# When blocks are closed, when an image's first keys are fetched, and where the routing's chain stands: three edits of order in a fused convolution, state-space, attention and expert kernel

## The chip, the cores and the metric

The kernel runs on one core of one Trainium2 chip. The metric is the device time of one execution in microseconds (us). Matrix products run on TensorE (PE), elementwise work and scans on VectorE (DVE), activations on ScalarE (ACT), a few powers and fills on GpSimd (POOL); SyncE (SP) issues the DMAs of the main loop.

## The reference, cut to what matters

Two layers over `x` of shape (4, 128, 64, 64): four images of 4,096 tokens with 128 channels, all in float32.

```python
# layer 0: group norm, depthwise 3x3 convolution, a Mamba scan over the tokens (4 chunks of channels)
x = x + conv_block(gn(x))
...
def step(h, inp):                       # for each of 4096 tokens
    dA_t, dBu_t, C_t = inp
    h = dA_t * h + dBu_t                # di = 64, N = 16
    y = jnp.einsum('bdn,bn->bd', h, C_t)
    return (h, y)
...
# layer 1: attention with 4 heads of 32, then 8 experts of which 2 are taken
t = to_tokens(x)
t = t + attention(ln(t))                # softmax(q k^T / sqrt(128)) v, then W_proj
n = ln(t)
p = softmax(n @ router_w + router_b)
top_p, top_i = top_k(p, 2);  top_p = top_p / sum(top_p)
t = t + sum_k top_p[k] * (n @ expert_w[top_i[k]] + expert_b[top_i[k]])
```

## The kernel before, in words

All of it is one loop (L1362) whose order is written out by hand. The program is built by Python generators; each engine's instructions are chained in the order in which they are recorded (`queued`, L389), so the order is fixed when the program is built and does not depend on time.

An image's tokens are cut into 8 blocks of 512 (`BLK`), so there are 32 blocks, (image b, block i). The scan of a block takes 2 halves of the channels (p) times 8 pairs of states; each such unit takes two turns of the loop, called steps here (`slot`). A block of the scan is thus 32 steps, and the scan ends after step 1,023. Block number k begins at step 32k. A step issues the fetch of the scan's rows from DRAM, one `da` activation for a later unit, in an even step the product `h` and the scan, in an odd step the product `hc`, and the transposes `y` of an earlier one.

Beside the scan, each step takes one attention group if there is one (L1383): two tiles of 128 keys against 1,024 queries of one head, 4 matmuls into `sc`, two exponentials into `pT`, and, in the next step, the matmuls into `av`. The groups of an image come from `attention(b)` (L912): the runs in `RUNS` (L903) name a pair of query blocks and a range of key blocks, each run goes over the four heads, and is cut into parts of one or two key blocks. A part is loaded (`qs`, `ks`, `v`, from DRAM) during the last three groups of the part ahead of it (L954) if all blocks that it needs are closed (`ready`, L908); if that was not so, the generator gives None, a step without a group, until they are, then loads, and gives None twice more (L940 to L945). There is one generator for each image, and they run one after the other (L1333): the first part of an image always takes the second way. An image has 256 groups.

Everything else runs in two lanes, X and Y, each with a queue of tasks; a task is a generator whose pieces are recorded at two places of a step. The Y lane gives its pieces in the middle of a step (L1393, L1406), the X lane one at the end of a step (L1412) and one early in the next (L1382), ahead of the attention group and of the scan or `hc`. An X task begins at the end of a step. Y has the group norm, the first norm (`gn`, `y0`), the convolution (`xn`, on VectorE as nine taps for images 1 to 3) and the scan's inputs (`in`, which also use the X lane's PSUM bank for two products). X has two kinds of task:
- `closed(b, i)` (L793): after the scan of a block it makes the layer's output, normalises it, and writes keys, queries and values to DRAM. It takes 18 pieces, and is put at the head of X when the second half of the block has been summed up (`summed_up`, L778). That is early in step 3 of the block that follows.
- `("out", b, i)` (`finished`, L1032): after all keys of a pair of query blocks, it loads the sums (`aT`), the inverse denominators (`inv`) and the tokens (`acc`), projects, normalises, routes, and adds the 8 experts' products, whose weights (shares) come back from DRAM. It takes 30 pieces; it is put at the tail of X by the third of the steps of `inverted`, 8 steps after the last group of the pair.

A task, once begun, keeps its lane to its end. As long as the scan runs, an output may begin only in steps 2 to 17 of a block (L1268). Before the change the outputs of a steady block begin in step 2, so the closed task that comes in step 3 waits for piece 30 and begins in step 17.

In `finished`, the router's exponential is piece 12, piece 13 is empty, the choice of the two experts (17 small instructions on VectorE, called the routing's chain) is piece 14, and the transposes of `both` on TensorE are piece 15. Odd pieces stand at the end of a step, even ones early in the next. Each lane has one PSUM bank (`ps_X`, `ps_Y`). After the scan, outputs may begin in any step and on both lanes.

Of the kernel before, what the change touches and what calls it, by code (L numbers as in the profile page):

```python
# [24 lines left out]
NST = 16  # L25
# [11 lines left out]
def conv_mamba_attn_moe_kernel(ctx: ExitStack, tc: tile.TileContext, t: dict):  # L37
    nc = tc.nc
    x, out = t["x"], t["out"]
    B, _, L = x.shape  # L40
    NB = L // BLK
# [11 lines left out]
    def load(name, shape=None, src=None, eng=nc.sync, pool=const):  # L53
        src = t[name] if src is None else src
        w = pool.tile(list(shape or src.shape), F32, name=f"w_{name}")
        eng.dma_start(out=w, in_=src)
        return w
# [354 lines left out]
    def mm(out, lhsT, rhs, start=True, stop=True):  # L412
        tensor.matmul(out, lhsT=lhsT, rhs=rhs, start=start, stop=stop)
# [460 lines left out]
    def queries(b, qp, h):  # L874

        qs = att.tile([P, 2 * BLK], F32R, name="qs", bufs=2)
        src = kqv[b][1][qp][DH * h : DH * h + DH].rearrange("d a r l -> (d a r) l")
        sync.dma_start(out=qs.bitcast(F32), in_=src)
        return qs

    def keys(b, h, k, u, n):

        ks = att.tile([P, 2 * BLK], F32R, name="ks", bufs=3)
        src = kqv[b][0][k][DH * h : DH * h + DH].rearrange("d a l -> (d a) l")
        src = src[:, u * BLK : (u + n) * BLK]
        sync.dma_start(
            out=ks[:, : n * BLK].bitcast(F32),
            in_=src[:, None, :].to_broadcast([2 * DH, 2, n * BLK]),
        )
        return ks  # L890

    def values(b, h, k, u, n):
        v = att.tile([P, 2, NT, 2 * DH], F32, name="v", bufs=3)
        sync.dma_start(
            out=v[:, :n].rearrange("p i j d -> p i (j d)"),
            in_=kqv[b][2][k][h, u : u + n].rearrange("i p q -> p i q"),
        )
        return v
# [9 lines left out]
    def ready(b, part):  # L908
        last = max(2 * part[0] + 1, 2 * part[2] + part[3] + part[4] - 1)
        return all(("closed", b, i) in done for i in range(last + 1))  # L910

    def attention(b):  # L912

        seen, parts = {}, []
        for q, lo, hi in RUNS:
            known = seen.get(q, 0)
            seen[q] = known + hi - lo  # L920
            cuts = [lo, *range(lo + 2 - lo % 2, hi, 2), hi]
            for h in range(NH):
                for k0, k1 in zip(cuts, cuts[1:]):
                    parts.append((
                        q, h, k0 // 2, k0 % 2, k1 - k0, k0 == lo, k1 == hi, known > 0,
                        seen[q] == NB,
                    ))
        assert all(n == NB for n in seen.values())

        def load(part, qs=None):  # L930
            q, h, k, u, n = part[:5]
            if qs is None:
                qs = queries(b, q, h)
            return qs, keys(b, h, k, u, n), values(b, h, k, u, n)

        prev = None
        ahead = None
        for at, part in enumerate(parts):
            q, h, k, _, n, first, last, more, final = part
            if ahead is None:  # L940
                while not ready(b, part):
                    yield None
                ahead = load(part)
                for _ in range(2):
                    yield None  # L945
            qs, ks, v = ahead
            ahead = None
            for g in range(0, NT * n, STEP):
                if g == 0 and last:
                    prev = None  # L950
                    if more:
                        prev = att.tile([P, BLK], F32, name="prev", bufs=2)
                        sync.dma_start(out=prev, in_=partial.pop((b, q, h)))
                if g >= NT * n - 3 * STEP and ahead is None and at + 1 < len(parts):  # L954
                    nxt = parts[at + 1]
                    if ready(b, nxt):
                        ahead = load(nxt, qs if nxt[:2] == (q, h) and not nxt[5] else None)
                scs = []
                for j in range(g, g + STEP):
                    sc = ps_sc.tile([P, 2, BLK], F32, name="sc")  # L960
                    for u in range(2):
                        mm(
                            sc[:, u, :], ks[:, j * P : (j + 1) * P],
                            qs[:, u * BLK : (u + 1) * BLK],
                        )
                    scs.append((v[:, j // NT, j % NT, :], sc))
                yield (
                    b, q, h, scs, first and g == 0, last and g + STEP == NT * n, prev, final,
                )
# [62 lines left out]
    def finished(b, qb, lane):  # L1032

        q, u = divmod(qb, 2)
# [44 lines left out]
        yield  # L1079
        scalar.activation(pr, pr, AF.Exp)  # L1080
        yield
        yield

        revb = rev[:, None, :].to_broadcast(wide)

# [16 lines left out]
        vector.reciprocal(top1, top1)  # L1102
        vector.tensor_mul(both[:, :, 0:NE], pr, top1.to_broadcast(wide))
        vector.tensor_mul(both[:, :, NE:], both[:, :, 0:NE], rs[:, :, None].to_broadcast(wide))
        yield

        ps = work(lane)
# [9 lines left out]
        def share(e):  # L1117

            if lane == "X":
                w = side.tile([P, 2, BLK], F32, name="share", bufs=3)  # L1120
            else:
                w = mix.tile([P, 2, BLK], F32, tag="rows", name="share", bufs=4)
            sync.dma_start(
                out=w.rearrange("p k q -> p (k q)"),
                in_=shares[e : e + 2].rearrange("e q -> (e q)")[None].to_broadcast([P, 2 * BLK]),
            )
            return w
# [8 lines left out]
        ahead = deque(share(e) for e in (0, 2))  # L1136
# [117 lines left out]
    def advance(lane, second):  # L1254

        if inside[lane] != second:
            return False
        while True:
            if lane not in running:

                tasks = lanes[lane] if lanes[lane] or slot < END else lanes["X"]
                if tasks and lane == "Y" and tasks[0][0][0] == "closed":
                    return False
                if not tasks or not all(k in done for k in tasks[0][2]):
                    return False

                if (
                    tasks[0][0][0] == "out" and slot < END + 4  # L1268
                    and not 2 <= slot % (2 * NST) < NST + 2
                ):  # L1270
                    return False
                key, stages, _ = tasks.popleft()
                running[lane] = key, stages(lane) if callable(stages) else stages
            key, stages = running[lane]
            try:
                next(stages)
                inside[lane] = not second
                return True
            except StopIteration:
                assert not second  # L1280
                done.add(key)
                del running[lane]

    def until(key):
        while key not in done:
            flush()
            count = len(done)
            moved = [
                advance(*half) for half in (("X", True), ("Y", False), ("Y", True), ("X", False))
            ]  # L1290
            assert any(moved) or len(done) > count, key
            if ("y0", *blocks[1]) in done:
                next(weights, None)
# [17 lines left out]
    for k in range(-2, len(blocks)):  # L1311
        if 0 <= k:
            b, i = blocks[k]
            Y.append((("in", b, i, 1), inputs(b, i, 1), [("scan", *blocks[k - 1], 1)] if k else []))
        if k + 2 < len(blocks):
            b, i = blocks[k + 2]
            if k + 2 == 0 or i > 0:
                upper(k + 2)
        if 0 <= k + 1 < len(blocks):
            b, i = blocks[k + 1]  # L1320
# [10 lines left out]
    left = [None]  # L1331

    def attention_groups():  # L1333
        for b in range(B):
            yield from attention(b)
        left.clear()

    groups = attention_groups()
    units = [(b, i, p, n) for b, i in blocks for p in range(2) for n in range(0, NST, 2)]
    END = 2 * len(units)  # L1340

    rows, due, closing, y_of = {}, deque(), deque(), {}
    h_of, slot = {}, 0
# [18 lines left out]
    while (  # L1362
        slot < END or due or closing or summing or waiting or left or later or lanes["X"] or running
    ):
        at, odd = divmod(slot, 2)
# [10 lines left out]
        if unit and not odd:  # L1376
            h = h_of.pop(at)
            driven(unit, h, rows.pop((at, 0)))
        if summing:
            summed_up(*summing)  # L1380
            summing = None
        advance("X", True)  # L1382
        group = next(groups, None)  # L1383
        if group:
# [3 lines left out]
        if unit and odd:  # L1388
            hc = read(h, rows.pop((at, 1)))
            late = 2 * (unit[3] == 0)  # L1390
            due.append((slot + 1 + late, unit, 0, hc[:, 0, :], False))
            due.append((slot + 2, unit, 1, hc[:, 1, :], ends(unit)))
        advance("Y", False)  # L1393
        while closing and closing[0][0] <= slot:
            summing = turned_back(*closing.popleft()[1:])
# [133 lines left out]
```

## Time and profile before

| | |
|---|---|
| three runs | 5178.62, 5182.59, 5191.08 us (median 5182.59) |
| the profiled execution | 5183.13 us, of which the span of the profile 5180.9 us |
| granted TensorE clock, mean | 0.957 |
| attention groups, `pT` exponentials | 1,024, 2,048 |
| `pT`, mean of one on ScalarE | 1022 ns |
| scan on VectorE, mean of one | 2353 ns |
| `h`, `hc` on VectorE, mean of one | 1218, 1220 ns |
| HBM read and written | 967.22 MB, 143.39 MB |

Times on the page are of one profiled execution. Instructions of the main loop all carry the line of the helper that records them (L406), so they are told apart by tile names: `sc` and `av` are attention, `h`, `hc`, `y`, `da` the scan, `both` the routing, `share` the experts' weights, `hi` and `lo` the keys and queries of a closed task, `gn`, `xt`, `cm` the norms and the convolution. A name with X or Y at its end belongs to a lane. The page gives each engine's busy time and 40 slices of the span:

```profile
PE   4567898999999998899999999999999999999997
DVE  6987767877778887878788887888788877751332
ACT  4556777787787787688888787788777787656543
PEclk7778999999999999899999999999999999999998
```

The first quarter is image 0, where attention starts late; the last four or five slices come after the scan has ended and hold attention and outputs alone.

### The profile page before, as it was taken

How to read it: one execution, taken by the hardware profiler on the slowest of the kernel's cores; microseconds unless marked ns; L12 is line 12 of the kernel's file. 1: busy time of each engine (PE TensorE's matmuls, PEld its weight loads, DVE VectorE, ACT ScalarE, POOL GpSimd, SP SyncE). 2: the span in 40 equal slices, each digit the busy share in tenths (PEclk: the TensorE clock that was granted, in tenths of full speed). 3: DMA queues.
4: the chain of work that ended last, by engine and by line, in shares of the span. 5: the costliest groups of instructions: out<-in, count | busy, mean ns of one | idle time of the engine just before them, and what ended most of it. 6: DMA issues, size and time to landing. Idle time of an engine off the chain costs nothing.

```text
span 5180.9 us, 62597 instructions
## 1 busy us (share of the span) xinstructions
PE 4710.1 (91%) x20684; PEld 2321.9 (45%) x20684; DVE 3835.8 (74%) x5780; ACT 3745.7 (72%) x5700; POOL 423.1 (8%) x483
## 2 busy tenths in 40 slices
PE   4567898999999998899999999999999999999997
PEld 2334444444444444444444444444444444443443
DVE  6987767877778887878788887888788877751332
ACT  4556777787787787688888787788777787656543
POOL 1111111100000000101000000000000001000000
PEclk7778999999999999899999999999999999999998
DMA  3556667677666766767766766777766666754542
GB/s 127 183 186 212 205 212 253 233 239 243 229 224 225 239 227 234 242 230 258 252 228 227 238 229 231 258 231 255 265 227 233 221 230 221 262 179 156 184 134 72
DMA packets 451693, 1131.70 MB, mean 218 GB/s; under 512 B 51858, under 2 KB 135331, under 8 KB 451363
## 3 DMA queue, kind: packets, MB, share of 16 engines
q1 hardware_dynamic: 447296, 1125.96, 64.3%
q8 instruction: 166, 2.72, 0.2%
q10 hardware_dynamic: 4066, 1.67, 0.1%
q14 instruction: 165, 1.34, 0.1%
HBM read 967.22 MB, written 143.39 MB: 214 GB/s over the span
## 4 chain that ended last, share of the span: by engine, by line
PE 59%; DVE 19%; ACT 10%; DMA 6%; issue 4%; POOL 2%; SPq 1%; DVEq 0%; ACTq 0%; POOLq 0%
PE av L406 25%; PE sc L406 14%; PE ps_X L406 9%; DVE h L406 6%; PE ps_Y L406 6%; PE y L406 5%; ACT pT L406 3%; ACT L406 2%; DVE hc L406 2%; DMA ks<-kd 2%; ACT xt L406 1%; DVE stX L406 1%; DVE du L406 1%; DMA rows<-bcd 1%; DVE cm L406 1%
## 5 line engine op out<-in xcount | busy, mean ns | idle before, releaser
L406 ACT ACTIVATE pT<-sc 128x1024 f32<-128x1024 f32 x2048 | 1984.3, 1022 | 934.3 <-PE sc L406 932.8
L406 PE MATMUL av<-pT,v 128*64 128x512 f32 x8192 | 2002.8, 610 | 10.8 <-DVE avs L406 10.8
L406 PE MATMUL sc<-qs,ks 128*128 128x512 f32 x4096 | 1302.7, 437 | 75.9 <-ACT pT L406 39.4
L406 DVE TENSOR_TENSOR_SCAN h<-da,state,h 128x1025 f32<-128x1025 f32 x512 | 1204.5, 2353 | 96.6 <-ACT h L406 62.8
L406 PEld LDWEIGHTS sc<-qs,ks 128*128 128x128 f32 x4096 | 703.1, 190 | 812.7 <-ACT pT L406 273.2
L406 PEld LDWEIGHTS av<-pT,v 128*64 128x64 f32 x8192 | 500.4, 137 | 845.7 <-issue 816.7
L406 ACT ACTIVATE da<-delta,amat 128x512 f32<-128x512 f32 x1024 | 742.9, 730 | 1.9
L406 PE MATMUL y<-ident,hc 128*128 128x128 f32 x4096 | 626.2, 284 | 64.6 <-DVE hc L406 64.6
L406 DVE TENSOR_TENSOR hc<-rows,h 128x1024 f32<-128x1024 f32 x512 | 624.6, 1220 | 15.3 <-PE y L406 5.4
L406 DVE TENSOR_TENSOR h<-rows,du 128x1024 f32<-128x1024 f32 x512 | 623.9, 1218 | 13.0 <-DMA rows<-bcd 8.5
L406 PEld LDWEIGHTS y<-ident,hc 128*128 128x128 f32 x4096 | 524.2, 147 | 229.0 <-issue 80.8
L406 ACT ACT_TABLE_LOAD x319 | 409.3, 1283 | 19.5 <-DVE zs L406 14.3
L406 POOL TENSOR_TENSOR rsX<-rsX,mhalf 128x4 f32<-128x4 f32 x92 | 203.7, 2214 | 2504.4 <-DVE rsX L406 2420.4
L406 POOL TENSOR_TENSOR rsY<-rsY,mhalf 128x4 f32<-128x4 f32 x100 | 130.7, 1307 | 2072.5 <-DVE shiftY L406 1561.5
L406 DVE TENSOR_TENSOR avs<-av,prev 128x512 f32<-128x512 f32 x96 | 66.2, 689 | 256.7 <-PE av L406 235.0
L406 PE MATMUL ps_X<-share,w_ew 128*128 128x512 f32 x432 | 213.9, 617 | 9.1 <-DVE share L406 8.8
L406 ACT ACTIVATE xt<-ps_Y,shiftY,rsY 128x128 f32<-128x128 f32 x380 | 143.6, 468 | 81.7 <-POOL shiftY L406 73.8
L406 DVE TENSOR_TENSOR share<-share,xf 128x1024 f32<-128x1024 f32 x128 | 156.0, 1219 | 16.5 <-DMA share<-sharesX 11.7
L406 ACT COPY state<-h 128x2 f32<-128x2 f32 x448 | 88.8, 198 | 92.0 <-DVE h L406 92.0
L406 DVE SCALAR_TENSOR_TENSOR cm<-y,w_fc1w,cm 128x512 f32<-128x512 f32 x195 | 145.1, 744 | 8.0 <-ACT y L406 4.5
L406 PE MATMUL ps_Y<-pairs,inxc 128*128 128x512 f32 x256 | 132.6, 643 | 15.5 <-DMA pairs<-xn 9.9
L406 PEld LDWEIGHTS ps_X<-share,w_ew 128*128 128x128 f32 x432 | 73.2, 189 | 147.0 <-issue 97.1
(248 smaller groups left out, 3437.2 us busy)
## 6 DMA issues: line engine op xcount, KB each, us to landing
rows<-bcd SPq DMA_DIRECT2D x1024, 512.0 KB
ks<-kd SPq DMA_DIRECT2D x192, 512.0 KB
qs<-qd SPq DMA_DIRECT2D x161, 512.0 KB
share<-sharesX SPq DMA_DIRECT2D x108, 512.0 KB
v<-vd SPq DMA_DIRECT2D x192, 256.0 KB
ks<-kd SPq DMA_DIRECT2D x128, 256.0 KB
avd<-avs SPq DMA_DIRECT2D x96, 256.0 KB
prev<-avd SPq DMA_DIRECT2D x96, 256.0 KB
```

Of the source, the lines that this page charges most:

```text
L406: return lambda *args, **kw: queued(op(*args, **kw))
```

## The change

Three edits. The generators of the images become one: `parts_of(b)` lists the parts of an image, `attention()` goes over the parts of all images, and each part carries its image, so the first part of an image can be loaded during the last groups of the image ahead of it by the same rule as any other. In the routing, the empty piece ahead of the chain is taken out and one is put behind it, so that the chain is piece 13 and the transposes stay piece 15. The steps in which an output may begin while the scan runs become 4 to 17.

```diff
-    def attention(b):
+    def parts_of(b):
...
                     parts.append((
-                        q, h, k0 // 2, k0 % 2, k1 - k0, k0 == lo, k1 == hi, known > 0,
-                        seen[q] == NB,
+                        b, (q, h, k0 // 2, k0 % 2, k1 - k0, k0 == lo, k1 == hi, known > 0,
+                            seen[q] == NB),
                     ))
         assert all(n == NB for n in seen.values())
+        return parts
+
+    def attention():
+
+        parts = [part for b in range(B) for part in parts_of(b)]
 
-        def load(part, qs=None):
+        def load(b, part, qs=None):
...
-        for at, part in enumerate(parts):
+        for at, (b, part) in enumerate(parts):
...
-                    nxt = parts[at + 1]
-                    if ready(b, nxt):
-                        ahead = load(nxt, qs if nxt[:2] == (q, h) and not nxt[5] else None)
+                    to, nxt = parts[at + 1]
+                    if ready(to, nxt):
+                        ahead = load(to, nxt, qs if nxt[:2] == (q, h) and not nxt[5] else None)
...
         scalar.activation(pr, pr, AF.Exp)
         yield
-        yield
 
         revb = rev[:, None, :].to_broadcast(wide)
...
         vector.tensor_mul(both[:, :, NE:], both[:, :, 0:NE], rs[:, :, None].to_broadcast(wide))
+        yield
         yield
...
                     tasks[0][0][0] == "out" and slot < END + 4
-                    and not 2 <= slot % (2 * NST) < NST + 2
+                    and not 4 <= slot % (2 * NST) < 18
...
     def attention_groups():
-        for b in range(B):
-            yield from attention(b)
+        yield from attention()
         left.clear()
```

More of the change, by code (lines that the diff above doesn't have):

```diff
@@ L942, in attention @@
                     yield None
-                ahead = load(part)
+                ahead = load(b, part)
                 for _ in range(2):
```

## The prediction

> **What bounds the kernel now.** I read the page first, then the busy time of TensorE in stretches of 32 steps, then TensorE's waits, then single places in the timeline. On the page TensorE is busy 91% of the span and leads the chain that ended last:
>
> ```profile
> PE 4710.1 (91%) x20684; PEld 2321.9 (45%) x20684; DVE 3835.8 (74%) x5780; ACT 3745.7 (72%) x5700; POOL 423.1 (8%) x483
> PE 59%; DVE 19%; ACT 10%; DMA 6%; issue 4%; POOL 2%; SPq 1%; DVEq 0%; ACTq 0%; POOLq 0%
> ```
>
> Each step issues one `da` activation (two more ahead of step 0), so the start of a 32-step block can be read off the timeline of `da`; counting the turns of the loop tells which steps have an attention group. Busy time in such stretches (us; TensorE busy; granted clock; DMA share; GB/s):
>
> ```profile
> 1219.70:1375.30 155.60, 143.91 (x642) 0.97 0.74 255
> 1664.40:1804.90 140.50, 126.03 (x567) 0.95 0.71 236
> 1804.90:1948.30 143.40, 140.00 (x642) 1.00 0.69 230
> 1948.30:2104.40 156.10, 129.79 (x544) 0.86 0.75 258
> 2249.70:2393.80 144.10, 140.47 (x642) 1.00 0.72 244
> 2393.80:2532.70 138.90, 131.44 (x600) 0.99 0.76 259
> 2825.40:2968.50 143.10, 134.55 (x618) 1.00 0.66 223
> 2968.50:3113.40 144.90, 141.45 (x647) 1.00 0.70 240
> 3113.40:3269.40 156.00, 143.50 (x630) 0.96 0.74 258
> 4001.80:4145.00 143.20, 135.30 (x613) 0.99 0.67 224
> 4145.00:4290.60 145.60, 140.89 (x642) 1.00 0.68 234
> 4690.00:4800.00 110.00, 110.00 (x443) 1.00 0.47 158
> ```
>
> An ordinary block (blocks 13, 16, 21, 29: 143.4, 144.1, 144.9, 145.6; mean 144.5) has 140 to 141 us of TensorE work and some 3.5 us in which it waits. So nothing is gained unless a wait of TensorE goes. The last row is a stretch after the scan has ended: attention alone, never idle; its groups follow each other every 2.99 us. The waits of TensorE from 1219.7 to 4559.3 us (total, times, longest) begin so:
>
> ```profile
> PE ps_X L406 <- DVE bothX L406: 40.0, 20, 4.1
> PE sc L406 <- ACT pT L406: 23.1, 87, 1.4
> PE sc L406 <- DMA ks<-kd: 21.1, 12, 4.7
> PE ps_X L406 <- DVE lo L406: 17.4, 20, 2.6
> ```
>
> **Part one: the groups that move (an image's first keys; closed tasks at step 3).** Counting the loop's turns in both programs: before, attention gives no group in steps 383-384, 409-412, 469-476, 653-654 and 911-912, 18 in all; two at each change of image (L944), the others because a block was not closed. After, there is none of these, since the closed task starts at step 3 of a block in place of 17. The last group falls in step 1150 in place of 1168; the loop has 1,176 turns for 1,194. Matmuls, exponentials and loads are the same in number.
> - Gained: 18 tail steps of 2.99 us = -53.8.
> - Paid: the same 18 groups inside the scan's steps. Block totals price them: block 12 (five bare steps, 384 and 409-412) took 140.5 against 144.5, so 4.0; block 11, with one, 142.5, so 2.0; blocks 20 and 28 143.1 and 143.2, so 1.4 and 1.3; block 14, with eight, took 156.1, and block 22, which has the same group norm and no bare step, 156.0: nothing. Together +8.7. The upper bound is from step to step: the 18 bare steps took 54.9 us (`da` to `da`), the same places of ordinary blocks some 83 by the means of 17 blocks: +28.
> - Sum -45.1, between -54 and -26. What goes is idle time in the bare steps, of which this wait (timeline) and this stretch at half clock (windows) are examples:
>
> ```profile
> 1793.21 1.11 PE L406 MATMUL y<-ident,hc 128*128 128x128 f32 x4 [6.67 <-DVE hc L406]
> 1666.40:1669.80 3.40, 3.13 (x10) 0.50 0.91 328
> ```
>
> **Part two: the routing's chain.** The chain (17 instructions on VectorE; in the timeline 1703.83 to 1707.37, 3.55 us) stood in step 9 after the VectorE work of step 8, and the transposes of `both` at the end of step 9 waited for it, 40.0 us in 20 blocks. Outputs now start at step 12 of the block, so the chain is queued at the end of step 18 and the transposes at the end of step 19. From the start of step 18 VectorE has `h` 1.22 + scan 2.35 + chain 3.55 = 7.1 us; TensorE has two steps of 3.42 (sc 1.2, y 0.6, av 1.94, overlapping) + `xt` 0.66 + `yT` 0.60 + fc2 1.2 = 9.3. The wait goes: -40.0, bounds -40 and 0. Without the moved yield `scanned` (0.73 + 0.69) would stand ahead: 8.5, still inside, so the half step alone is worth nothing here. On POOL the closed task's two powers move to steps 6 and 7 and the output's to 15; POOL is busy 8%, so only its latency counts, as in `xt` below. On SP's queue the output's share loads keep their distance to its own steps. Behind the chain on VectorE now stand `scanned` and `hc` of step 19 (done after 7.1 + 1.42 + 1.22 = 9.7); `hc` is read in step 20, after 9.3 + 0.65 + 1.2, and nobody waits.
>
> **Part three: what the closed task brings to steps 3 to 12.** Blocks 8, 9 and 17 have that order already. All three show the same stall in step 8:
>
> ```profile
> 2429.52 1.20 PE L406 MATMUL sc<-qs,ks 128*128 128x512 f32 x4
> 2432.81 0.66 PE L406 MATMUL ps_Y<-ident,gn 128*128 128x128 f32 x4 [2.09 <-DVE gn L406]
> ```
>
> In step 7 the closed task's `tt` and moments (2428.71 to 2431.08) and `hc` stand ahead of `gn`. There are 17 changed blocks with a `gn` there: 17 x 2.09 = +35.5 (0 if TensorE is later by then). The waits for `lo` (17.4), which come from closed tasks meeting `inputs` in steps 24 to 26, go, less 6.2 already counted in bare blocks: -11.2. In step 18 TensorE waits for `xt` 1.2 to 1.9 in the three blocks; the output's router matmuls (29.4 us / 27 = 1.09) now fill part of it: 0.5 x 20 = +10 (0 to 24). In blocks 14, 22, 30 VectorE has taps in steps 6 to 10; the 4.05 of `both` there is in the 40.0, and the closed task's 3.2 us of moments takes its place, up to 6 us: 3 x 3 = +9 (0 to 18).
>
> **Part four: just in time, and the clock.** The run that begins 80 groups into an image needs queries whose closed task ends in step 460, 716 or 972; they are asked for one step later and used in 463, 719, 975. Loads of `ks` took 7.05 and 8.15 us in the chain, after a write that must land first, against four steps of 3.4: +6, 0 to 15. As to the clock, each 3.4 us at half rate costs 1.7: `both` was followed by three such windows (4 in units of 3.4, -6.8), one stall for `gn` of three was (1260.2 to 1263.6, clock 0.50), so 17/3 x 1.7 = +9.6: +3 (0 to 20).
>
> [...]
>
> **Sum.** -45.1 - 40.0 + 35.5 - 11.2 + 10 + 9 + 6 + 3 = -32.8, on a profiled execution of 5183.1 (span 5180.9), which stands 0.5 above the median of the runs. Predicted: 5182.6 - 32.8 = 5149.8, taken as 5150. Likeliest case alone: 5122 to 5166. What a measurement of this kernel can tell from no change is about 0.3%, 15.5 us.
>
> **Rivals.**
> - *The exchange of order costs what the closed gaps give* (0.17). TensorE idles 8.4 and 7.5 us in blocks 8 and 17, which have the new order, against 3.5 in ordinary ones, without an output to carry. If the changed blocks idle 2 us more than before instead of my net 0.6 (12.3 / 22), 22 x 2 = 44 eats the 45: 5181.
> - *Slower: the output's first loads* (0.08). `aT`, `inv`, `acc` are issued after `hc` of step 11, and `aT x inv` waits for them on VectorE with the scan of step 14 behind it. Issue to product took 8.8 to 12.6 us; before, the steps 3 to 5 with `inputs` (5.3 us of TensorE) hid it, now steps 12 to 14 have three bare 3.42 = 10.3. At 4817.15 the same wait cost TensorE 4.09. It decides from landings of about 12 us on: 22 x 4.09 = 90, so 5182.6 - 33 + 90 = 5240. Against it: VectorE itself has two taps of 0.74 in step 11, then 1.2 + 0.7 + 2.35 + 1.5 in step 12, 1.2 + 1.5 in 13 and `h` 1.2 in 14, 11.1 us, before it gets there. On SP's queue the fetch of `rows` for step 13 stands behind these three loads, 0.5 us each to issue.
> - *More gain* (0.10, faster too): `gn` hidden and bare groups free, -54 - 40 - 11 = -105 at the most; half of the difference to mine gives 5114.
> - *The chain still waits* (0.05, within 0.3%): +40 on mine, 5190; the half step then did not do what it says. Against it stands the margin of 2.2 us above.
> - The forecast: 0.60. Faster than 5167: 0.60 + 0.10 + a part of the first rival (0.04) = 0.74; within 5167 and 5198: 0.13 + 0.05 = 0.18; slower: 0.08. The range for 8 in 10: 5116 (between more gain and mine) to 5181.
>
> **What would show it.** No step without a group after step 206: `pT` to the end of the scan without holes, and the attention-only stretch shorter by about 54 us. `bothX` gone from TensorE's waits before 4500 us; `gn` in them with some 17 x 2.1. If `aT` or `hc` leads them instead, the loads are the cause and I am wrong; if ordinary blocks stay near 144.5 and the time still falls by under 20, part one is mis-priced.

## The result and the profile after

| | before | after |
|---|---|---|
| median of six runs, us | 5186.30 (5178.62 to 5195.01) | 5235.73 (5234.73 to 5249.21) |
| span of the profiled execution | 5180.9 | 5232.3 |
| TensorE busy, its 20,684 matmuls | 4710.1 | 4728.6 |
| TensorE idle (span less busy) | 470.8 | 503.7 |
| start of the scan's last `da` | 4568.0 | 4681.6 |
| from there to the end of the span | 612.9 | 550.7 |

The ratio after to before is 1.0101, 95% interval 1.0086 to 1.0116: slower by 1% (below, a point is 1% of the time before, some 52 us). The forecast was 5150, and the range ended at 5181. The span grew by 51.4 us: the part after the scan became 62.2 shorter, as forecast in kind, but the scan became 113.6 longer. Seen from TensorE, 32.9 us are more idling and 18.5 us are the same matmuls taking longer.

The page after, its busy row and the shares of the chain that ended last. VectorE's share of the chain fell from 19% to 16%, and that of DMA rose from 6% to 9%:

```profile
PE 4728.6 (90%) x20684; PEld 2330.4 (45%) x20684; DVE 3835.0 (73%) x5780; ACT 3739.6 (71%) x5700; POOL 461.1 (9%) x483
PE 60%; DVE 16%; DMA 9%; ACT 8%; issue 3%; POOL 3%; SPq 1%; ACTq 0%; DVEq 0%; POOLq 0%
```

TensorE in stretches of 32 steps after the change (stretch; its length; TensorE busy; granted clock; DMA share; GB/s), here blocks 12, 13, 14, 16, 17, 20, 21, 28 and 29:

```profile
1677.30:1824.60 147.30, 141.84 (x642) 0.99 0.68 233
1824.60:1973.30 148.70, 141.87 (x637) 0.98 0.68 230
1973.30:2133.10 159.80, 145.78 (x642) 0.96 0.77 257
2284.00:2432.30 148.30, 140.82 (x637) 0.99 0.73 248
2432.30:2587.70 155.40, 143.66 (x642) 0.98 0.74 257
2887.80:3034.40 146.60, 140.71 (x642) 1.00 0.69 233
3034.40:3183.80 149.40, 141.76 (x637) 0.98 0.67 230
4106.20:4253.30 147.10, 140.67 (x642) 1.00 0.69 233
4253.30:4401.70 148.40, 139.36 (x637) 1.00 0.68 230
```

The blocks with closed bare steps (12, 14, 20, 28) rose by 6.8, 3.6, 3.4 and 4.0 us. The ordinary ones shown (13, 16, 21, 29) had no bare step to pay for and rose as much: by 5.3, 4.2, 4.5 and 2.8. Block 17 rose by 16.5, because an output now falls into it. So the loss is not the price of the groups that moved; nearly every block pays it.

TensorE's waits from 1219.7 to 4559.3 us after the change (total, times, longest); the stretch holds blocks 9 to 30, and before the change nearly all of block 31 as well:

```profile
PE ps_Y L406 <- DVE gn L406: 39.7, 19, 2.1
PE sc L406 <- DMA ks<-kd: 38.3, 12, 5.5
PE ps_X L406 <- DVE aT L406: 38.1, 17, 4.2
PE sc L406 <- ACT pT L406: 12.9, 44, 1.4
PE ps_Y L406 <- ACT g L406: 12.6, 19, 1.1
PE ps_Y L406 <- DVE cm L406: 12.3, 12, 1.6
```

In the same stretch before:

```profile
PE ps_Y L406 <- DVE gn L406: 6.4, 5, 2.1
...
PE ps_X L406 <- DVE aT L406: 0.4, 2, 0.2
```

`g` had 0.2 and `cm` 1.1 there. The 40.0 of `bothX` and the 17.4 of `lo` are gone. `gn` is the stall that the forecast named; `aT` is the one that it named as the sign that the loads are the cause.

What a stall costs shows in the timeline of TensorE after the change, in step 8 of block 13 (start; duration; instruction; in brackets the idle time before it and what ended it):

```profile
1858.97 1.20 PE L406 MATMUL sc<-qs,ks 128*128 128x512 f32 x4
1862.25 0.66 PE L406 MATMUL ps_Y<-ident,gn 128*128 128x128 f32 x4 [2.09 <-DVE gn L406]
1862.74 0.76 PE L406 MATMUL y<-ident,hc 128*128 128x128 f32 x4
1863.44 3.42 PE L406 MATMUL av<-pT,v 128*64 128x512 f32 x8
```

The eight `av` matmuls behind the 2.09 us gap take 3.42 us in place of 1.94 (eight others, at 1857.10). The stretch at that place and another one, behind an `aT` stall, with the columns as above:

```profile
1863.00:1866.40 3.40, 3.40 (x12) 0.51 0.72 216
1893.80:1897.20 3.40, 3.40 (x13) 0.50 0.48 190
```

TensorE is busy throughout both, at half its clock (0.51 and 0.50). The loss of a block is therefore split into its idle time and its half-rate time. The table gives the mean of the nine blocks that are ordinary in both kernels (13, 15, 16, 19, 21, 23, 24, 27, 29). Half-rate time is summed from stretches of 1.7 us as twice the missing clock, and half of it, at a granted clock of 0.50, is lost. The kernels of the experiments are included, for use below; each row is of one execution:

```
                              length  idle  half-rate time   (us per block)
before                         144.4   3.7   0.0
e2_merge                       144.0   3.7   0.4
e3_chain                       144.3   3.7   0.0
e9_split                       144.5   3.3   0.4
e8_late                        144.7   3.6   0.4
e14_before_nomom               145.1   4.1   0.0
e12_z22                        147.5   5.5   1.1
e13_loads_nomom                147.7   6.3   2.3
e10_nomom                      147.6   5.9   3.0
e1_gate                        148.4   6.6   2.7
e5_loads                       148.9   6.9   4.6
e11_z20                        148.9   6.4   4.9
e7_both                        149.2   7.1   4.2
after                          149.7   7.0   6.1
e4_nochain                     149.7   6.9   6.8
e6_gn                          151.6   8.7   4.2
e15_mom9                       153.2   8.5   9.5
```

An ordinary block idles 3.4 us more (before rounding) and loses another 3.0 to the clock. What is left of its busy time without that loss is 1.1 us less than before, for a reason that is not shown. That makes 5.3 in all, where the forecast had a net 0.6.

### The profile page after: what moved, and what is told of

It is laid out like the page before. It is cut to its first block, busy times and chain, and to the rows that moved or that the text cites. A ratio compares the mean times of both kernels' runs of the same rounds, so it can differ in the third digit from the quotient of the medians.

```text
span 5232.3 us, 62572 instructions
## 1 busy us (share of the span) xinstructions
PE 4728.6 (90%) x20684; PEld 2330.4 (45%) x20684; DVE 3835.0 (73%) x5780; ACT 3739.6 (71%) x5700; POOL 461.1 (9%) x483
## 4 chain that ended last, share of the span: by engine, by line
PE 60%; DVE 16%; DMA 9%; ACT 8%; issue 3%; POOL 3%; SPq 1%; ACTq 0%; DVEq 0%; POOLq 0%
PE av L406 25%; PE sc L406 14%; PE ps_X L406 9%; PE ps_Y L406 6%; PE y L406 6%; DVE h L406 5%; DMA inv<-inverse 3%; ACT pT L406 3%; DMA ks<-kd 2%; POOL rsX L406 2%; DVE hc L406 2%; ACT L406 2%; DMA rows<-bcd 2%; DVE stX L406 1%; DVE du L406 1%
## 5 line engine op out<-in xcount | busy, mean ns | idle before, releaser
L406 DVE TENSOR_TENSOR res<-res,ps_X 128x512 f32<-128x512 f32 x108 | 74.0, 685 | 205.5 <-PE ps_X L406 205.2
L406 ACT ACTIVATE xt<-tt,shiftX,rsX 128x128 f32<-128x128 f32 x128 | 52.7, 482 | 136.8 <-POOL shiftX L406 136.8
L406 DVE TENSOR_TENSOR cm<-ps_X,cm 128x512 f32<-128x512 f32 x32 | 22.1, 692 | 170.0 <-PE ps_X L406 170.0
```

What stands on the lines that cost most here:

```text
L406: return lambda *args, **kw: queued(op(*args, **kw))
```

## The experiments

**Each edit alone.** Which of the three edits costs the time? First the gate alone, in the kernel before (e1_gate):

```diff
-                    and not 2 <= slot % (2 * NST) < NST + 2
+                    and not 4 <= slot % (2 * NST) < 18
```

> The kernel before with the gate edit alone (outputs begin in steps 4 to 17, so closed tasks come first; six steps without a group are left, two at each change of image). Theory A, the exchange of order carries the loss through new stalls of TensorE (gn 2.09 in 17 blocks, aT about 2.2 in 17, each followed by a stretch at half clock): 5240 to 5255 us, gn near 40 and aT near 38 in TensorE's waits. Theory B, the merged list of parts carries it, its early key loads crowding the others: 5150 to 5186.

Measured: ratio 1.0055 (1.0038 to 1.0072), between the two expectations. This edit brings a loss, though only about half of it. Against the gate alone, the whole change has 28.7 us less behind the scan (579.4 to 550.7), but its scan ends 43.0 us later (4638.6 to 4681.6). The gate's waits lead with the same names and `pT`:

```profile
PE sc L406 <- DMA ks<-kd: 37.8, 13, 5.1
PE ps_Y L406 <- DVE gn L406: 33.6, 18, 2.1
PE sc L406 <- ACT pT L406: 21.5, 57, 3.7
PE ps_X L406 <- DVE aT L406: 21.2, 15, 3.2
```

Here `aT` has 21.2 us, against 38.1 with all three edits.

Then the merged list of parts alone, in the kernel before (`attention()` and `parts_of` of the change, nothing else; e2_merge):

> The kernel before with the merged list of parts alone (14 steps without a group after step 206 in place of 18; the loop has 1,190 turns). Theory A: 5172 to 5186, the four tail steps of 2.99 us less what four groups cost in the scan. Theory B: 5220 to 5240.

Measured: 0.9991 (0.9982 to 1.0001), some 5 us less, with an interval from 9 less to no change. In the profiled execution the scan's end came 7.2 us later and what follows became 6.2 shorter. So the four steps closed by this edit are worth little in the old order.

The chain half a step sooner, alone in the kernel before (e3_chain, the edit shown), and the whole change with the chain put back (e4_nochain):

```diff
         scalar.activation(pr, pr, AF.Exp)
         yield
-        yield
...
         vector.tensor_mul(both[:, :, NE:], both[:, :, 0:NE], rs[:, :, None].to_broadcast(wide))
+        yield
         yield
```

> The kernel before with the routing's chain half a step sooner alone. In the old place (end of step 8 in place of early in step 9) no instruction of VectorE stands between the two places, so theory A: 5178 to 5194, bothX still near 40 us in TensorE's waits. Rival: bothX goes and the time falls to 5140 to 5155.

> The changed kernel with the chain put back (merged list and gate stay). Theory A: 5228 to 5245, as the changed kernel; bothX under 6 us before 4500 us, since the wait left with the outputs' new place and not with the half step. Rival: the chain ahead of scanned is what delays hc and cm (waits of fc2 for g and of the transposes for cm, 24 us together): 5205 to 5222.

Measured: 0.9997 (0.9988 to 1.0007) for the chain alone, and 1.0089 (1.0072 to 1.0106) for the change without it, where `bothX` is not among TensorE's waits before 4500 us either. No worth of the half step is seen in either order.

The merged list does little in the old order, but the change without the chain (gate and list) is 0.34 points slower than the gate alone; the two intervals just touch. The trace shows what the list does there. SyncE's queue in the change, in step 12 of block 13 (issue time; duration of the issue; transfer):

```profile
1879.80 0.90 SPq L406 DMA_DIRECT2D qs<-qd  x1
1880.75 0.54 SPq L406 DMA_DIRECT2D ks<-kd  x1
1881.38 0.55 SPq L406 DMA_DIRECT2D v<-vd  x1
1881.98 0.46 SPq L406 DMA_DIRECT2D aT<-total  x1
1882.49 0.55 SPq L406 DMA_DIRECT2D inv<-inverse  x1
```

And what waits for it, VectorE's product and the projection on TensorE; ahead of them, the `hc` of step 11:

```profile
1877.93 1.21 DVE L406 TENSOR_TENSOR hc<-rows,h 128x1024 f32<-128x1024 f32 x1
...
1892.93 0.69 DVE L406 TENSOR_TENSOR aT<-aT,inv 128x512 f32<-128x512 f32 x1 [3.39 <-DMA inv<-inverse]
...
1893.68 2.03 PE L406 MATMUL ps_X<-w_wp,aT 128*128 128x128 f32 x8 [2.83 <-DVE aT L406]
```

An attention part's 512 KB loads of `qs` and `ks` are issued just ahead of the output's loads. VectorE idles 3.39 us for `inv`, and behind that TensorE idles 2.83. Of the 22 outputs of the changed kernel that begin in blocks 10 to 31, eleven have both `qs` and `ks` among the three loads right ahead, with a mean wait at the projection of 2.8 us; six have one of them, 1.2 us; five none, 0.26 us. The difference lies mostly in when the output's loads are issued: `inv` goes out a median of 3.7 us after the end of the last `hc` with both ahead and 1.9 us with none, while from there to the product it takes 10.5 and 9.9 us. In the kernel with the gate alone only 2 of 21 have both, and these two stand ahead of its first steps without a group (383 and 384). Without such steps the parts' starts fall on the outputs' first step. That is a correlation; the next run takes the wait away.

**The two stalls.** The output's product `aT` x `inv` one step later, behind its own loads, in the changed kernel (e5_loads):

```diff
         yield
+        yield
+        yield
         vector.tensor_mul(aT, aT, inv)
```

> The changed kernel with the output's product aT x inv and all behind it one step later than its loads (two more empty pieces). Theory A, TensorE stands behind the loads of an output begun in step 12, 38 us in 17 blocks, with some 13 windows of 3.4 us at half clock behind them, 1.7 us each: 5175 to 5192, aT gone from TensorE's waits before 4560 us, gn unchanged near 40. Rival: the wait is DMA crowding and moves with the loads: 5225 to 5245.

Measured: 1.0075 (1.0058 to 1.0092), 0.26 points less than the change, between the two expectations; the two intervals overlap a little (1.0086 to 1.0092). Its waits begin:

```profile
PE sc L406 <- DMA ks<-kd: 42.2, 11, 6.2
PE ps_Y L406 <- DVE gn L406: 39.9, 19, 2.1
PE ps_Y L406 <- ACT xt L406: 33.8, 33, 2.3
PE ps_X L406 <- DVE share L406: 16.6, 18, 1.3
```

The 38.1 of `aT` are gone, but `xt` went from 3.5 to 33.8 and `share` from 5.7 to 16.6, so only about 13 us of time came back.

The transposes of `gn` one step later, in the changed kernel, alone (e6_gn) and together with the edit above (e7_both):

```diff
         yield
+        yield
+        yield
         ps = transposed(lane, by_tile(gn))
```

> The changed kernel with the transposes of gn (and the Y lane behind them) one step later than gn (two more empty pieces). Theory A, the stall behind gn, 40 us and ten windows at half clock, 17 us, is the closed task's place in step 7: 5175 to 5195, gn gone from TensorE's waits, aT near 38 or less. Rival: the stall turns into another of the Y lane's (cm, xt, g), which wait for VectorE just as well: 5220 to 5240.

> Both of the edits of the two runs ahead of this one on the changed kernel. Theory A, two separate stalls that add: 5115 to 5145, under the kernel before. Rival, VectorE is the bound of the new order and any stall taken away comes back elsewhere: 5180 to 5235.

Measured: 1.0159 (1.0137 to 1.0181) for `gn` alone and 1.0057 (1.0040 to 1.0074) for both. The first is slower than even the rival allowed; its waits begin:

```profile
PE y L406 <- DVE hc L406: 44.6, 31, 1.9
PE ps_X L406 <- DVE aT L406: 35.7, 15, 3.8
```

The 39.7 us for `gn` became 44.6 for `hc`: what is late is VectorE, with the closed task's moments, and if one instruction of TensorE no longer waits for it, the next one does. With both edits `hc` has 36.9, `ks` 44.2 and `cm` 32.7. Why the `gn` edit costs 0.58 points alone and nothing on top of the other is not shown.

The next kernel therefore shortens VectorE's work in place of moving the wait. It is the change with the closed task's second moments left out (four `bn_stats` and four `bn_aggr` a block; another factor stands in, and keys, queries and values differ; e10_nomom):

```diff
-        xt = yield from normalised("X", tt)
...
+        vector.tensor_scalar_add(ra, rs, EPS)
+        vector.tensor_scalar_mul(shift, rs, -1.0)
+        gpsimd.tensor_tensor(ra, ra, mhalf, ALU.pow)
...
```

> The changed kernel without the closed task's second moments (4 bn_stats and 4 bn_aggr, 1.3 us of VectorE in step 7; the normalisation takes another factor, so the output differs). Theory V: the stall for gn falls from 2.09 to about 0.8 and no other grows, 5200 to 5218. Rival, the place of gn and not VectorE's load makes the stall: 5228 to 5245.

Measured: 1.0047 (1.0031 to 1.0064). Its row for `gn`:

```profile
PE ps_Y L406 <- DVE gn L406: 17.4, 19, 1.0
```

The stall shrinks from 2.1 to 0.9 us each, and the half-rate time of the ordinary blocks halves with it (6.1 to 3.0): 0.54 points. The same edit in the kernel before, as a control (e14_before_nomom):

> Control: the kernel before without the closed task's second moments (output differs). Theory S, the 34 us were the stall of step 7 in the new order, and in the old order the moments (step 21) keep nobody waiting: 5174 to 5186. Rival G, TensorE is slowed by VectorE's amount of work anywhere: 5145 to 5160.

Measured: 1.0008 (0.9998 to 1.0018). Leaving the moments out of their old place gains nothing, so the 0.54 points are what their new place costs. Both cures together, `aT` later and no moments, in the changed kernel (e13_loads_nomom):

> The changed kernel with both the later use of the output's loads and without the closed task's second moments (output differs). If the two stalls are separate causes and add: 5236 - 17 - 34 = 5185, between 5178 and 5192. If VectorE takes back what one stall gives up: 5200 to 5215.

Measured: 1.0011 (1.0001 to 1.0020). Apart the two give back 0.26 and 0.54 points, together 0.90 of the 1.01.

The next one leaves the moments in but puts them behind `gn` and `hc` of step 7, half a step later, while the activations that need them stay where they were (nothing left out; e15_mom9):

```diff
-        xt = yield from normalised("X", tt)
+        yield
+        mv, rt = moments("X", tt)
...
```

> The changed kernel with the closed task's second moments one piece later, at the end of step 7 behind hc and gn in place of ahead of them; nothing left out. Theory S: gn falls to about 17 us in TensorE's waits, 5200 to 5218, as without the moments. Rival: the late normalisation makes TensorE wait for xt in step 8 instead: 5225 to 5245.

Measured: 1.0302 (1.0285 to 1.0320), far worse than expected, though `gn` fell as it should:

```profile
PE ps_X L406 <- ACT xt L406: 59.2, 22, 3.5
PE ps_X L406 <- DVE aT L406: 39.1, 18, 4.0
...
PE ps_Y L406 <- DVE gn L406: 15.0, 19, 1.1
```

Now the closed task's own `xt` is late: behind the moments stands a power on GpSimd (2.97 us at 1886.34), its four activations come after that, and they have half a step less.

**The wait for `both`.** The forecast's largest credit after the tail was these 40 us. Taken away in the old order: the transposes one step later (e8_late), and then one step later with the chain split in two pieces (e9_split). Both edits make the output a step longer, so the closed task also begins in step 18 and one more step has no group (19 in place of 18):

```diff
         vector.tensor_mul(both[:, :, NE:], both[:, :, 0:NE], rs[:, :, None].to_broadcast(wide))
         yield
+        yield
+        yield
```

> The kernel before with the transposes of both one step later than the chain (two empty pieces behind it; closed tasks then begin in step 18, 19 steps without a group in place of 18). Theory A, a stall of TensorE of 1.85 us in a block is worth itself and its clock, in the old order as in the new: bothX 40 us gone, about 7 us of clock, one tail step of 3 us more: 5136 to 5150. Rival: another wait takes its place: 5175 to 5190.

```diff
         top1, pick1 = largest(pr, 1)
+        yield
         rest = routed("rest")
...
         vector.tensor_mul(both[:, :, NE:], both[:, :, 0:NE], rs[:, :, None].to_broadcast(wide))
         yield
+        yield
```

> The kernel before with the routing's chain in two halves (early in step 9 and at its end) and the transposes of both one step later; closed tasks begin in step 18. Theory V, a burst of VectorE's work in one step is the bound there, and only spreading or shortening it helps: neither bothX nor hc stays large in TensorE's waits (under 15 us each), 5150 to 5170. Rival, the stall goes to hc as in the run with the transposes late alone: 5190 to 5205.

Measured: 1.0032 (1.0021 to 1.0042) and 1.0020 (1.0010 to 1.0030); neither gains, and the first is slower than even its rival allowed. In the first `bothX` is gone and `hc` has 40.7 us. In the second the wait is nearly gone:

```profile
...
PE y L406 <- DVE hc L406: 14.6, 17, 5.8
PE ps_Y L406 <- ACT xt L406: 13.6, 17, 1.2
...
PE ps_X L406 <- DVE bothX L406: 4.0, 3, 1.3
```

Yet the ordinary blocks stay at 144.5 and their idle time falls by only 0.3 us: 1.8 us of `both` a block were replaced by other waits; those for `hc`, `xt`, `cm` and `ks` (21.1 to 30.8) grew. What the later closed task adds to the time of these two kernels was not measured apart.

**Another place for the outputs.** The changed kernel with the outputs begun in step 20 (e11_z20), and in step 22 of a block (e12_z22):

```diff
-                    and not 4 <= slot % (2 * NST) < 18
+                    and not 20 <= slot % (2 * NST) < 22
```

```diff
-                    and not 4 <= slot % (2 * NST) < 18
+                    and not 22 <= slot % (2 * NST) < 24
```

> The changed kernel with outputs begun in step 20 (gate 20 to 21), so that their routing and shares fall in steps 27 to 2, where the Y lane is empty; no step without a group. Theory V: the closed task's stall for gn stays (near 40), the loads' stall stays (aT 25 to 40), the rest of the output meets an idle VectorE: 5190 to 5220. Rival, the order closed first is not the cost: 5228 to 5245.

> The same with outputs begun in step 22 (gate 22 to 23): inputs in steps 24 to 26 cover the loads, and the closed task begins in step 5, away from the gn of step 7; two steps without a group. Theory V: aT under 10 and gn under 15 us in TensorE's waits, 5145 to 5180. Rival: 5220 to 5245.

Measured: 1.0080 (1.0059 to 1.0102) and 1.0029 (1.0016 to 1.0042), the second slower than theory V had it. Step 20 has next to no wait for `aT`, against what was expected, but `pT` 47.3 and `xt` 22.1 in its place, beside `gn` at 39.8. In step 22 the closed task begins in step 5 of the next block, past the collision:

```profile
PE ps_Y L406 <- ACT xt L406: 26.3, 32, 1.3
PE sc L406 <- ACT pT L406: 26.0, 83, 1.4
PE sc L406 <- DMA ks<-kd: 20.8, 9, 4.8
...
PE ps_Y L406 <- DVE gn L406: 4.0, 3, 2.1
```

`gn` and `aT` both go without any work being left out, `ks` is back at its old size, and some 70% of the loss with them. It stays slower than before: ordinary blocks 147.5, with many small waits. No kernel of the study is measurably faster than the kernel before.

## Why the prediction was wrong, step by step

| term of the sum | predicted, us | what the runs show |
|---|---|---|
| the end after the scan | -53.8 | -62.2, one output that moved into block 17 included |
| price of the 18 groups in the scan | +8.7 | not to be seen: blocks 12, 14, 20, 28 rose by a mean 4.5, the nine ordinary ones by 5.3 |
| wait for `both` | -40.0 | wait gone; taken away in the old order (e8, e9) it gained nothing |
| the half step itself | 0 | 0 (-0.03 points in the old order, interval -0.12 to +0.07) |
| `gn` | +35.5 | +33.3, and half-rate time behind it |
| `lo` | -11.2 | 17.4 gone |
| `xt` in step 18 | +10 | not there; `g` +12.4 and `cm` +11.2 were not priced |
| blocks 14, 22, 30 | +9 | block 14 rose by 3.6, no more than others |
| `ks` just in time | +6 | +17.2; the three named loads 12.2 of it (3.99, 3.91, 4.27) |
| the output's first loads | 0 | +37.7 (`aT`) |
| clock | +3 | +18.5 of longer matmuls |

Three steps of it failed.

*The credit for `both`.* "The wait goes: -40.0" was right for the wait and wrong for the time. The margin of 2.2 us was computed correctly, and `bothX` is indeed gone; but when it was taken away in the old order (e8, e9), the ordinary blocks idled 3.6 and 3.3 us in place of 3.7, behind other waits, and the time did not fall. The prediction's bounds were -40 and 0, and it took the end for which these runs give no support.

*The output's loads at nothing.* The rival set 12 us from issue to landing as the point of decision, and the forecast relied on 11.1 us of VectorE's own work as cover. Both figures were near. Issue to product took a median of 10.36 us in the change, against 9.83 before, and VectorE had a median of 10.4 us of own work from the end of the last `hc` ahead until it stood idle. But the one is counted from the issue of `inv` and the other from `hc`, and the time between the two was left out. In the rows shown, `hc` ends at 1879.14 and `inv` is issued at 1882.49, 3.35 later, behind `qs`, `ks` and `v`; the product starts another 10.44 later, at 1892.93, of which VectorE stood idle for 3.39. What the forecast did not look at was which loads stand right ahead on SyncE's queue, and that the merged list puts `qs` and `ks` there. The mean wait was 1.8 us (39.7 / 22, over the whole scan), not the 4.09 of the one row used as price.

*The clock.* The term counted one half-rate window for three stalls of `gn` and three such windows saved with `both`. In the trace of before, the eleven waits for `both` of 1.17 to 1.85 us have none behind them; the nine ordinary blocks have no half-rate time at all. Of the six longer ones (2.02 to 4.06 us) five have. The waits for `gn`, 2.08 to 2.11, have one in 11 of 19 cases, and those for `aT` in 9 of the 12 over 1 us. The change swapped cheap gaps for slightly longer, dearer ones.

With these three terms mended (0, +37.7, +18.5) the sum of -32.8 becomes -32.8 + 40 + 37.7 + 15.5 = +60.4, against the measured +51.4. The three are put in as measured, and other terms were off as well (-8.4 at the end after the scan, +23.6 for `g` and `cm`), so the closeness proves little. That the slower rival's figure of 5240 lies close to the result is a coincidence of its sum: it had the mechanism, but at 90 us for the loads alone. Taking the wait for the loads away (e5) gives back 0.26 points, some 13 us; the place of the moments (e10, with e14 as control) 0.54, some 28; both together 0.90. The rival "the exchange of order costs what closed gaps give" was right in kind: 3.4 us more idling a block, where it needed 2.

Right were: that no bare step is left after 206 and the end shrinks accordingly; the stall for `gn` in place, size and number; `lo`; the half step at nothing. The clue was on the table: blocks 8 and 17, which already had the new order, idled 8.4 and 7.5 us against 3.5, and the forecast set its own net of 0.6 above that.

Open stay three things. Why an ordinary block of the old order keeps some 3.5 us of idling when the wait for `both` is taken away. What the closed steps are worth by themselves: by the merged list alone four of them gave some 5 us (0 to 9), where the step price of the forecast (45.1 / 18 = 2.5) asks for 10 us. And what holds the ordinary blocks of e13 and e12 3.2 us above the old ones once `gn` and `aT` are cured, which their shorter ends after the scan (549.5 and 565.9 us against 612.9) hide in the time; in e13 `ks` (39.9) and `xt` (34.0) lead the waits, and no run took these away.

## What to carry to other kernels

A stall of the bounding engine behind another engine named a late engine here, not a removable cost: putting the waiting instruction (e6, e8) or the work that it waits for (e15) later moved the wait to the next one, while less work ahead of it (e10) did help; more time for a load (e5) gave back a third of the wait. A load's time is counted from where the program asks for it, with the issues ahead of it on its queue, and compared with a cover that starts at the same point. An exchange of order is priced by blocks that already have the whole new order, its loads and their neighbours on the queue included; if such blocks are slower, the burden is on the forecast to show why the others will not be. And a gap is priced with the clock behind it: in these traces the eleven waits for `both` of 1.17 to 1.85 us had no half-rate stretch behind them, while 11 of the 19 for `gn` of 2.1 us had one, 3.4 us at a clock of 0.50, which is another 1.7 us.

## What the runs showed of the hardware

*Half clock behind a stall.* Of TensorE's stalls from 1220 to 4560 us, the table counts those with a granted clock under 0.6 within 4.8 us of their end. In the kernel before, one of the 6 and five of the 19 began when the clock was already halved:

```
idle of TensorE     before      after
1.0 to 1.9 us      6 of 29     3 of 28
1.9 us and over   19 of 23    33 of 42
```

One `both` from the small side, in the kernel before, with the stretch behind it at full clock:

```profile
1849.72 0.60 PE L406 MATMUL ps_X<-ident,bothX 128*16 128x128 f32 x4 [1.79 <-DVE bothX L406]
```

```profile
1849.80:1853.20 3.40, 3.40 (x22) 1.00 0.25 82
```

In these traces no sharp length parts the stalls with half clock behind them from those without: of the waits for `gn` in the changed kernel, 2.08 to 2.11 us long, 11 of 19 have a half-rate stretch behind them.

*GpSimd's small power.* On 128x4 elements it took 2.22 us as a mean over the 92 of lane X and 1.36 over the 100 of lane Y, in the profile of the changed kernel. Four activations and then TensorE stand behind it in a closed task, so in e15 its latency comes on top of the moments'; how much of that kernel's loss it holds was not measured apart.
